# The end of a self-attention phase: exponentials, context work and the next LayerNorm in another order

## The chip, the cores and the metric

The kernel runs on one core of a Trainium2 chip. The metric is the device time of that core in microseconds, from runs that are not profiled; the median of three runs of the kernel before is 2554.23 us (2554.19 to 2556.33). One further execution was recorded by the profiler; all times inside the kernel come from that one.

## What is computed

Two transformer blocks follow each other on `x` of 8 x 512 x 512 in float32 (B = 8 sequences of N = 512 rows and H = 512 columns, 16 heads of 32), with a context of 8 x 77 x 512. Cut to what matters here (biases left out):

```python
# block 1 (phase "x"): cross attention of x to the context, adaptive LayerNorm
x = x + attention(ada_ln(x) @ Wq, ada_ln(ctx) @ Wkv) @ Wp
# block 2, phase "a": self-attention with modulation and a gate
q, k, v = split((ln(x) * (1 + scale_a) + shift_a) @ W_qkv)
x = x + gate_a * (softmax(q @ k.T * 32 ** -0.5) @ v @ W_proj)
# block 2, phase "c": cross attention to the context again
q_c = ln(x) @ W_qc
k_c, v_c = split(ln(ctx) @ W_kvc)
x = x + softmax(q_c @ k_c.T * 32 ** -0.5) @ v_c @ W_cproj
# block 2, phase "m": MLP 512 -> 2048 -> 512 with gelu, modulation and gate
```

The change lies where phase "a" ends and phase "c" begins.

## The kernel before

The four phases run one after the other. `x` lives in DRAM between them, one tensor per phase and sequence (`xa_b`, `xc_b`); in SBUF there are three slots of 128 x 4 x 512 (the pool `xres`), and `next_x` (L143 to L149) loads the next sequence in a fixed order into the next slot. Two of the three slots hold the running sums of exponentials (`sums`, `sum_a` in the profile) through the self-attention. The first load of phase "c", `x_c`, takes the slot of the first sum.

**Order of the work.** In phase "a" every engine's instructions keep the order in which the Python text makes them (`tc.manual_schedule(engines=None)`). Each engine takes its own in that order and waits by semaphores. The loads and stores that are issued from SyncE (SP) keep their order too, those of GpSimd (POOL) stand among POOL's additions, and two weight loads are issued from ScalarE (ACT). In phase "c" the compute engines keep the written order as well.

**Self-attention.** The work is cut into 32 groups: one sequence and four heads each (`Group`, L973). Per group the score tiles S^T are made (128 keys x 4 heads x 512 queries, four tiles k = 0 to 3, each in two halves of 128 x 1024), copied to SBUF as `e_a`, and the maxima go through DRAM (`spread`, L1027). Then:

- `shift(k)` (L1042): POOL issues for each half of tile k a DMA that adds the negated maxima, read from DRAM and broadcast, onto `e_a`. 512 KB are read and written for each half, eight halves for a group.
- `exp(k)` (L1052): ACT takes the exponential of both halves in place (L1054).
- `add_up(k)` (L1056): running sum of the tiles, on POOL for k = 1 and 2 and on VectorE (DVE) for k = 3 (L1061).
- `outputs(k)` (L1065): 4 products of `e_a` with the values into `o_ps_a` in PSUM (L1071).
- `total` and `finish` (L1078, L1087): sum over keys by a product with ones (L1082), reciprocal (L1089) and product (L1092), which gives `oT_a`.

`project(b, t)` (L952) makes row tile t of the output projection: 4 products (L302), a bias addition on DVE that frees the PSUM tile (L960), and through `flush` two operations on POOL (L963, L964) and a store from SP (L967).

**Context work beside it.** `ContextC` makes the keys and values of the context for phase "c": `values(t)`, five row tiles (L349), each copied from PSUM by ACT (L354) and stored to DRAM by SP (L355); after the fifth, one load from SP brings all values back as `cv_c` with 77 partitions (L467). `keys(j)` (L469) makes a block of the keys in two pieces (512 and 104 columns, L473) with an ACT evacuation each (L478). All these, the projection and `total` share two PSUM banks (tag `m`) in turn.

**The last group.** Groups overlap inside the main loop. The last one, of sequence 7, has nothing behind it, and its steps are written out by hand after the loop, beside values 2, 3 and 4 and keys 0 and 1 of the context. `g` is this group, `prev` the one before it, `past` the one before that. `next_x(nc.sync)` loads `x_c` of sequence 0. `ln_rows` (L252) is the LayerNorm of phase "c" for it, a generator with these pieces: statistics of row tiles 0 and 1 (L259, L260); of tiles 2 and 3; the first six small operations of the inverse root (L221 to L230); the rest of them with the offset (L243); then four ACT operations that normalise one row tile each (L248). `ln_T` of phase "c" then transposes the rows on TensorE (`lnT_ps_c`, L281), with a copy by ACT for each block (L283), and phase "c" goes on with keys 2 of the context and the first queries (`s_ps_qc`, L510).

The lines that put each wait into the code are few:

```python
# L469 keys(j): a yield after each product, the evacuation after the last
for at, n, cT in ((0, H, self.cT), (H, RL, self.last)):
    pk = ps_m.tile([P, H], F32, tag="m", ...)
    for k in range(KC):
        nc.tensor.matmul(pk[:, :n], lhsT=self.w_k[:, k, ts(j, P)], rhs=cT[:, k, :], ...)
        yield
    evac = nc.scalar.activation(self.kT[:, j, at : at + n], pk[:, :n], ...)
```

`values(t)` has one yield, between its products and its copy. `pump(gen, n)` takes n such steps, `run(gen)` takes the rest.

Of the kernel before, what the change touches and what calls it, by code (L numbers as in the profile page):

```python
# [29 lines left out]
def tile_pixart_block(ctx: ExitStack, tc: tile.TileContext, a: dict, out: bass.AP):  # L30
    nc = tc.nc
    x, ctx_in, cond = a["x"], a["ctx_1024"], a["cond_1024"]
    B, N, _ = x.shape
    S = ctx_in.shape[1]
    NT = N // P
# [13 lines left out]
    def load_w(name, u, rows=False, pool=wpool, queue=nc.sync):  # L49

        t = pool.tile([P, KC, H], F32, tag="w", name=f"w_{name}_{u}")
        w = a[name]
        src = w[ts(u, H), :] if rows else w[:, ts(u, H)]
        queue.dma_start(out=t, in_=src.rearrange("(k p) f -> p k f", p=P))
        return t
# [26 lines left out]
    gate_a = dram.tile([B, H], F32, name="gate_a")  # L82
# [6 lines left out]
    def run(gen):  # L89
        while True:  # L90
            try:
                next(gen)
            except StopIteration as stop:
                return stop.value
# [48 lines left out]
    def next_x(queue=nc.scalar):  # L143

        if len(x_sb) < len(x_order):
            ph, b = x_order[len(x_sb)]
            t = xpool.tile([P, NT, H], F32, tag="x", name=f"x_{ph}{b}")
            x_sb[ph, b] = t
            return queue.dma_start(out=t, in_=x_src[ph][b].rearrange("(t p) d -> p t d", p=P))  # L149
# [65 lines left out]
    def rsqrt_pieces(var, eps, nm, n):  # L215
        rows = var.shape[0]
        v = small.tile([P, CT], F32, tag="ln_v", name=f"lnv_{nm}")
        y = small.tile([P, CT], F32, tag="ln_y", name=f"lny_{nm}")
        t = small.tile([P, CT], F32, tag="ln_t", name=f"lnt_{nm}")
        v, y, t = v[:rows, :n], y[:rows, :n], t[:rows, :n]  # L220
        nc.vector.tensor_scalar(v, var, eps, None, ALU.add)  # L221

        nc.vector.tensor_scalar(
            y.bitcast(I32), v.bitcast(I32), -0.5, RSQRT_SEED, ALU.mult, ALU.add
        )
        nc.vector.tensor_scalar(v, v, -0.5, None, ALU.mult)
        for i in range(3):
            nc.vector.tensor_tensor(t, y, y, ALU.mult)
            nc.vector.tensor_tensor(t, t, v, ALU.mult)
            nc.vector.scalar_tensor_tensor(y, t, 1.5, y, ALU.add, ALU.mult)  # L230
            if i == 0:
                yield
        return y

    def normalise(dst, src, mv, y, i, rows):
        nc.vector.tensor_scalar(
            dst, src, mv[:rows, i, 0:1], y[:rows, i : i + 1], ALU.subtract, ALU.mult
        )

    def offsets(mv, y, n):  # L240

        off = small.tile([P, CT], F32, tag="off", bufs=2, name="off")[:, :n]
        nc.vector.scalar_tensor_tensor(off, mv[:, :n, 0], -1.0, y, ALU.mult, ALU.mult)  # L243
        return off

    def normalise_s(dst, src, off, y, i, rows):

        nc.scalar.activation(  # L248
            dst, src, AF.Identity, bias=off[:rows, i : i + 1], scale=y[:rows, i : i + 1]
        )  # L250

    def ln_rows(nm, b, eps, vector=False):  # L252


        xb = x_sb[nm, b]
        mv = small.tile([P, NT, 2], F32, tag="mv", name=f"mv_{nm}{b}")
        for t in range(NT):
            bn = small.tile([P, 6], F32, tag="st", name=f"st_{nm}{b}_{t}")
            nc.vector.bn_stats(bn, xb[:, t, :])  # L259
            nc.vector.bn_aggr(mv[:, t, :], bn)  # L260
            if t % 2:
                yield
        y = yield from rsqrt_pieces(mv[:, :, 1], eps, f"{nm}{b}", NT)
        off = offsets(mv, y, NT)
        yield
        for t in range(NT):
            if vector:
                normalise(xb[:, t, :], xb[:, t, :], mv, y, t, P)
            else:
                normalise_s(xb[:, t, :], xb[:, t, :], off, y, t, P)  # L270
            yield
# [27 lines left out]
    def mm_N(ps, w, xT, cols):  # L299

        for k in range(KC):
            nc.tensor.matmul(  # L302
                ps, lhsT=xT[k][:, cols], rhs=w[:, k, :], start=(k == 0), stop=(k == KC - 1)
            )
            yield

    def gate_rows(gate, b, pool, nm, bufs=2):
        g = pool.tile([P, H], F32, tag="gate", bufs=bufs, name=f"gate_{nm}{b}")
        nc.sync.dma_start(out=g, in_=gate[b].partition_broadcast(P))
        return g  # L310
# [28 lines left out]
    with tc.tile_pool(name="ps_s", bufs=2, space=PSUM, reuse_waits="tile") as ps_s:  # L339
# [539 lines left out]
        def self_phase(w, bo_row, work, work_2, ctx_c):  # L879
# [4 lines left out]
            st = [dict(xT=[], v={}, o=[], q={}, k={}, x={}) for _ in range(B)]  # L884
# [9 lines left out]
            def flush(part):  # L894

                while later[part]:
                    later[part].popleft()()
# [6 lines left out]
            def load_tile(b, t, queue=nc.scalar):  # L904
                xr = work.tile([P, H], F32, tag="xr", bufs=4, name=f"xr_a{b}_{t}")
                queue.dma_start(out=xr, in_=x_src["a"][b][ts(t, P), :])
                st[b]["x"][t] = xr
# [44 lines left out]
            def project(b, t):  # L952
                if t == 0 and b + 1 < B:
                    st[b]["g"] = gate_rows(gate_a, b, work, "a")
                pr = ps_m.tile([P, H], F32, tag="m", name=f"proj_ps_a{b}_{t}")
                for i, _ in enumerate(mm_N(pr, w_o, st[b]["o"], ts(t, P))):
                    if i == KC - 1:
                        xr = st[b]["x"].pop(t)
                        tmp = work.tile([P, H], F32, tag="res", bufs=3, name=f"res_a{b}_{t}")
                        nc.vector.tensor_tensor(tmp, pr, bo_row, ALU.add)  # L960

                        def add():
                            nc.gpsimd.tensor_tensor(tmp, tmp, st[b]["g"], ALU.mult)  # L963
                            nc.gpsimd.tensor_tensor(xr, xr, tmp, ALU.add)  # L964

                        def store():
                            nc.sync.dma_start(out=x_dst["a"][b][ts(t, P), :], in_=xr)  # L967

                        later[0].append(add)
                        later[1].append(store)  # L970
                    yield
# [136 lines left out]
            def pump(gen, n):  # L1108
                for _ in range(n):
                    next(gen, None)  # L1110
# [103 lines left out]
            g = groups[-1]  # L1214
# [16 lines left out]
            value = ctx_c.values(2)  # L1231
            next(value)
            prev.total()
            run(value)
            prev.finish()
            work_2.release()
            kv = tc.alloc_tile_pool(name="kv_c", bufs=1, side="right", reuse_waits="tile")
            ctx_c.room(kv)
            next_x(nc.sync)
            rows = ln_rows("c", 0, 1e-6)  # L1240
            fills = [ctx_c.values(3), ctx_c.values(4), ctx_c.keys(0)]
            for k in range(NT):
                g.exp(k)
                if k:
                    g.add_up(k)
                g.outputs(k)
                if k == 0:
                    st[g.b]["g"] = gate_rows(gate_a, g.b, work, "a")
                    for t in range(NT):
                        load_tile(B - 1, t, nc.sync)  # L1250
                if k < len(fills):
                    run(fills[k])
            w_c = [load_w("L1_xcond_W_qc", 0, queue=nc.scalar)]
            w_c.append(load_w("L1_xcond_W_cproj", 0, queue=nc.scalar))
            run(ctx_c.keys(1))
            g.total()
            g.finish()
            run(rows)
            for t in range(NT):
                run(project(B - 1, t))  # L1260
                flush(0)
                flush(1)
            return w_c, kv

        class Modulation:
# [66 lines left out]
        with tc.tile_pool(name="work_a", bufs=2, reuse_waits="tile") as work, tc.tile_pool(  # L1332
            name="ps_a", bufs=2, space=PSUM, reuse_waits="tile"
        ) as ps_m, tc.tile_pool(
            name="ps_o", bufs=2, space=PSUM, reuse_waits="tile"
        ) as ps_o, tc.manual_schedule(engines=None):
            w_l1 = [load_w("L1_xcond_W_qkv", u) for u in (2, 0, 1)] + [load_w("L1_xcond_W_proj", 0)]
            ctx_c = ContextC(load_w("L1_xcond_W_kvc", 1), work, c_mv)
            w_c, kv = self_phase(w_l1, load_row("L1_xcond_b_proj", 0, "bo"), work, work_2, ctx_c)
# [297 lines left out]
```

## Time and profile before

| what | value |
|---|---|
| median of three runs | 2554.23 us |
| the profiled execution's own time | 2556.85 us |
| its span, first to last instruction | 2555.1 us |
| granted TensorE clock, mean | 0.99 |
| phase "a", first to last product `o_ps_a` | 508.7 to 1344.2 us |
| exponentials of the last group begin | 1319.23 us |
| `oT_a` of the last group begins | 1353.73 us |
| projection tile 2 begins | 1360.72 us |
| first transposes of `x_c` (block 0) | 1367.26 us |
| first queries of phase "c" (`s_ps_qc`) | 1374.91 us |

The profile lists an instruction by line, engine, operation and tile (`out<-in`), with its start from the beginning of the span and its duration. PE is TensorE; PEld is its weight load, which can overlap; a float32 product shows as two records in this kernel, so four products of a projection tile are eight. A bracket `[1.68 <-DVE res_a L960]` says that the engine was idle for 1.68 us before the instruction, and what ended it. SPq, ACTq and POOL with DMA_DIRECT2D are issues of transfers, not the transfers.

### The profile page before, as it was taken

The page shows a single profiled execution, that of the slowest core. Times are in us where ns is not written, and L with a number is a line of the kernel's source. Part 1 is how long each engine was busy: PE and PEld are TensorE (multiplying, and loading weights), DVE is VectorE, ACT ScalarE, POOL GpSimd, SP SyncE. Part 2 cuts the span into 40 slices and gives each one's busy share as a digit, 9 for nine tenths or more (in the row PEclk, how much of TensorE's full clock was granted, in tenths as well). Part 3 has the DMA queues.
Part 4 walks back from the last instruction along what each step waited for, and adds up shares of the span by engine and source line. Part 5 has one row for each costly group of instructions (what it writes and reads, how often), then busy time and mean ns, then how long its engine had stood idle before and what let it go on. Part 6 is the DMA issues. An engine that isn't in the chain of part 4 may idle for free. (4 is left out here: it accounts for less than half of the span.)

```text
span 2555.1 us, 35387 instructions
## 1 busy us (share of the span) xinstructions
PE 2437.6 (95%) x13205; PEld 1562.6 (61%) x13205; DVE 1776.1 (70%) x3230; ACT 1224.9 (48%) x2083; POOL 1103.1 (43%) x982
## 2 busy tenths in 40 slices
PE   7999999989999999999988999998999999999998
PEld 3577776323333333333325777777888888888887
DVE  3588886478788888887756888887546545555553
ACT  1466665477676776767643666662121121121220
POOL 2245452277776877768663445445102102012011
PEclk9899999999999999999999999999999999999999
DMA  7323323499999899999995213133111011011010
GB/s 259 135 51 95 89 27 74 102 180 193 198 179 205 183 199 195 180 199 180 216 210 171 72 34 67 18 64 98 36 35 38 33 39 38 25 34 49 20 35 25
DMA packets 116676, 273.44 MB, mean 107 GB/s; under 512 B 12722, under 2 KB 29186, under 8 KB 116378
## 3 DMA queue, kind: packets, MB, share of 16 engines
q0 software_dynamic: 46368, 151.06, 33.0%
q1 hardware_dynamic: 64197, 108.37, 12.6%
q10 hardware_dynamic: 5941, 11.76, 1.3%
q8 instruction: 104, 1.70, 0.3%
q14 instruction: 66, 0.54, 0.1%
HBM read 234.78 MB, written 44.76 MB: 109 GB/s over the span
## 5 line engine op out<-in xcount | busy, mean ns | idle before, releaser
L1546 POOL TENSOR_TENSOR res_m<-res_m,gate_m 128x256 f32<-128x256 f32 x64 | 52.1, 814 | 665.1 <-DVE res_m L1544 665.1
L1045 POOL DMA_DIRECT2D e_a<-mxd_a x256 | 250.4, 2060 | 157.9 <-DMA mxd_a<-mxT_a 148.6
L1054 ACT ACTIVATE e_a<-e_a 128x1024 f32<-128x1024 f32 x256 | 265.1, 1058 | 98.4 <-DMA e_a<-mxd_a 98.0
L1009 ACT COPY e_a<-sT_a 128x1024 f32<-128x1024 f32 x256 | 254.2, 1010 | 91.0 <-DVE mx_a L1011 49.0
L1480 ACT ACTIVATE hT<-hT,bcol 128x512 f32<-128x512 f32 x128 | 91.9, 721 | 237.0 <-DVE hT L1455 228.9
L1061 POOL TENSOR_TENSOR sum_a<-e_a,e_a 128x1024 f32<-128x1024 f32 x64 | 150.2, 2363 | 105.8 <-ACT e_a L1054 105.4
L1011 DVE TENSOR_TENSOR mx_a<-sT_a,mx_a 128x1024 f32<-128x1024 f32 x128 | 150.9, 1216 | 33.6 <-PE sT_a L991 27.9
L1061 POOL TENSOR_TENSOR sum_a<-sum_a,e_a 128x1024 f32<-128x1024 f32 x64 | 171.2, 2686 | 5.3 <-ACT e_a L1054 5.3
L991 PE MATMUL sT_a<-qT_a,kT_a 32*128 32x512 f32 x1024 | 151.4, 640 | 17.7 <-ACT e_a L1009 16.1
L1071 PE MATMUL o_ps_a<-e_a,v 128*32 128x512 f32 x1024 | 152.9, 608 | 12.8 <-ACT e_a L1054 12.8
L1447 PE MATMUL q_ps_h<-x_m,w_L_xcond_W_mlp 128*128 128x256 f32 x512 | 132.3, 381 | 0.0
L1447 PE MATMUL q_ps_h<-xT_m,w_L_xcond_W_mlp 128*128 128x256 f32 x512 | 131.6, 380 | 0.0
L294 PE MATMUL q_ps_a<-xnT_a,w_L_xcond_W_qkv 128*128 128x512 f32 x256 | 124.1, 613 | 7.6 <-ACT xnT_a L914 7.6
L1089 DVE RECIPROCAL rz_a<-z_ps_a 128x512 f32<-128x512 f32 x32 | 107.4, 3357 | 31.9 <-PE z_ps_a L1082 31.9
L1447 PE MATMUL q_ps_h<-x_m,w_s 128*128 128x256 f32 x512 | 121.9, 381 | 5.3 <-DVE w_s L1401 4.6
L302 PE MATMUL proj_ps_a<-w_L_xcond_W_proj,oT_a 128*128 128x512 f32 x256 | 118.1, 605 | 3.1 <-DVE res_a L960 1.7
L294 PE MATMUL k_ps_a<-xnT_a,w_L_xcond_W_qkv 128*128 128x512 f32 x256 | 120.5, 608 | 0.0
L302 PE MATMUL v_ps<-w_L_xcond_W_qkv,xnT_a 128*128 128x512 f32 x256 | 119.7, 611 | 0.0
L991 PEld LDWEIGHTS sT_a<-qT_a,kT_a 32*128 32x128 f32 x1024 | 42.4, 183 | 117.7 <-ACT e_a L1009 51.9
L1447 PE MATMUL q_ps_y<-w_L_xcond_W_mlp,h_s 128*128 128x256 f32 x512 | 113.1, 379 | 0.0
L1447 PE MATMUL q_ps_y<-w_L_xcond_W_mlp,hT 128*128 128x256 f32 x512 | 113.1, 379 | 0.0
L1447 PE MATMUL q_ps_y<-w_t,h_s 128*128 128x256 f32 x512 | 111.8, 379 | 0.0
(368 smaller groups left out, 5531.1 us busy)
## 6 DMA issues: line engine op xcount, KB each, us to landing
e_a<-mxd_a POOLq DMA_DIRECT2D x256, 512.0 KB, 11.7
xa<-res_x POOLq DMA_DIRECT2D x32, 256.0 KB, 5.2
xr_a<-xa SPq DMA_DIRECT2D x32, 256.0 KB, 6.1
xc<-xr_a SPq DMA_DIRECT2D x32, 256.0 KB, 8.6
x_c<-xc SPq DMA_DIRECT2D x8, 1024.0 KB, 5.1
w_L_xcond_W_mlp<-in_L_xcond_W_mlp_dram SPq DMA_DIRECT2D x8, 1024.0 KB, 6.9
xc<-res_c POOLq DMA_DIRECT2D x32, 256.0 KB, 5.0
x_m<-xc SPq DMA_DIRECT2D x8, 1024.0 KB, 5.4
```

What stands on the lines that cost most here:

```text
L294: nc.tensor.matmul(ps, lhsT=w[:, k, ts(j, P)], rhs=xT[k], start=(k == 0), stop=(k == KC - 1))
L302: nc.tensor.matmul(ps, lhsT=xT[k][:, cols], rhs=w[:, k, :], start=(k == 0), stop=(k == KC - 1))
L991: nc.tensor.matmul(sc[h // 2][:, h % 2, :], lhsT=kT[ts(h, HD), ts(k, P)], rhs=qT[ts(h, HD), :], start=True, stop=True,)
L1009: nc.scalar.copy(self.e[k][i], sc[i])
L1011: nc.vector.tensor_tensor(self.mx[1 - i], sc[1 - i], self.e[0][1 - i] if k == 1 else self.mx[1 - i], ALU.max,)
L1045: nc.gpsimd.dma_start(out=self.e[k][i].rearrange("p h n -> p (h n)"), in_=self.mxd[2 * i : 2 * i + 2, :] .rearrange("h n -> (h n)").partit ...
L1054: nc.scalar.activation(self.e[k][i], self.e[k][i], AF.Exp)
L1061: engine.tensor_tensor(sum_i, self.e[0][i] if k == 1 else sum_i, self.e[k][i], ALU.add)
L1071: nc.tensor.matmul(self.po[ts(h, HD), :], lhsT=vt[:, self.fc * P + h * HD : self.fc * P + (h + 1) * HD], rhs=self.e[k][h // 2][:, h % 2, : ...
L1089: nc.vector.reciprocal(r, self.pz)
L1447: nc.tensor.matmul(self.banks[n][:, half], lhsT=lhsT, rhs=rhs, start=(k == 0), stop=(k == len(pairs) - 1),)
L1480: nc.scalar.activation(dst, src, AF.Gelu_apprx_tanh, bias=bias_cols("L1_xcond_b_mlp1", 1, j))
```

## The change

```diff
             value = ctx_c.values(2)
             next(value)
             prev.total()
+            g.exp(0)
             run(value)
             prev.finish()
             work_2.release()
             kv = tc.alloc_tile_pool(name="kv_c", bufs=1, side="right", reuse_waits="tile")
             ctx_c.room(kv)
+            g.outputs(0)
+            st[g.b]["g"] = gate_rows(gate_a, g.b, work, "a")
+            for t in range(NT):
+                load_tile(B - 1, t, nc.sync)
+            fills = [ctx_c.values(3), ctx_c.values(4), ctx_c.keys(0)]
+            for k, fill in enumerate(fills, 1):
+                pump(fill, 4 if k == 3 else 1)
+                g.exp(k)
+                g.add_up(k)
+                run(fill)
+                g.outputs(k)
             next_x(nc.sync)
-            rows = ln_rows("c", 0, 1e-6)
-            fills = [ctx_c.values(3), ctx_c.values(4), ctx_c.keys(0)]
-            for k in range(NT):
-                g.exp(k)
-                if k:
-                    g.add_up(k)
-                g.outputs(k)
-                if k == 0:
-                    st[g.b]["g"] = gate_rows(gate_a, g.b, work, "a")
-                    for t in range(NT):
-                        load_tile(B - 1, t, nc.sync)
-                if k < len(fills):
-                    run(fills[k])
             w_c = [load_w("L1_xcond_W_qc", 0, queue=nc.scalar)]
             w_c.append(load_w("L1_xcond_W_cproj", 0, queue=nc.scalar))
             run(ctx_c.keys(1))
             g.total()
             g.finish()
-            run(rows)
+            rows = ln_rows("c", 0, 1e-6)
             for t in range(NT):
+                next(rows)
                 run(project(B - 1, t))
                 flush(0)
                 flush(1)
+            run(rows)
             return w_c, kv
```

The change has three parts.

1. **Exponentials ahead of copies.** On ACT the four pairs of exponentials of the last group now stand one place earlier: exp(0) ahead of the copy of values 2, exp(1) ahead of that of values 3, exp(2) ahead of that of values 4, exp(3) ahead of both evacuations of keys 0. TensorE's order is as before.
2. **The load later.** `next_x`, the load of `x_c`, stands on SP's queue behind the load of the gate, the four loads of `xr_a`, the last two stores of context values and the load of `cv_c`, directly ahead of a weight load (`W_mod`). Before, it stood ahead of all of these.
3. **LayerNorm between the projection's tiles.** On DVE the statistics of rows 0 and 1, those of rows 2 and 3, the first half of the inverse root and its second half now stand ahead of the bias addition (L960) of projection tiles 0, 1, 2 and 3 respectively. Before, all four pieces stood ahead of the first. The normalisation on ACT stands behind the projection in both.

Nothing is added to or taken from what is computed.

## Prediction

> **What bounds the kernel now.** The page comes first. TensorE is busy nearly all the time, so a gain has to be idle time of TensorE that goes away. The windows view puts such time where phase "a" ends: in columns of PE, PEld, DVE, ACT and POOL busy time, PE has 12 us less work in the last stretch of 200 us than in the one before.
>
> ```profile
> PE 2437.6 (95%) x13205; PEld 1562.6 (61%) x13205; DVE 1776.1 (70%) x3230; ACT 1224.9 (48%) x2083; POOL 1103.1 (43%) x982
> ```
> ```profile
> 1000.00:1200.00 200.00, 190.59 (x817) 62.99 (x816) 164.84 (x188) 142.81 (x160) 150.11 (x106) 1.00 0.96 192
> 1200.00:1400.00 200.00, 178.55 (x769) 72.08 (x767) 130.22 (x165) 101.66 (x138) 121.17 (x91) 0.97 0.83 195
> ```
>
> The chain of waits, taken over this stretch, names the holes (start, duration, what):
>
> ```profile
> 1329.65 3.62 PE cv_ps_c L349 x8
> 1333.78 1.07 ACT e_a L1054
> 1334.89 2.00 PE o_ps_a L1071 x8
> 1336.89 4.52 PE ckT_ps_c L473 x16
> 1341.82 0.91 ACT e_a L1054
> 1342.78 2.00 PE o_ps_a L1071 x8
> 1344.78 4.50 PE ckT_ps_c L473 x16
> 1349.28 1.04 PE z_ps_a L1082 x8
> 1350.34 3.37 DVE rz_a L1089
> ...
> 1360.07 0.61 DVE res_a L960
> 1360.72 7.13 PE proj_ps_a L302 x16
> 1367.98 0.69 DVE res_a L960
> 1368.71 0.67 PE lnT_ps_c L281 x4
> ```
>
> Each block of context work is followed by an exponential that begins only after it, because ACT takes the copy of that block first. At 1360.72 the projection restarts after a bias addition that stood behind the LayerNorm on DVE.
>
> What the exponentials may wait for instead is the shift transfer. The tile view of `e_a` has eight, the last issued at 1317.7 and landing 21.2 us later, at 1338.9; the semaphore records give all eight: 1314.3, 1317.5, 1323.0, 1325.8, 1329.0, 1332.3, 1335.6, 1338.9.
>
> ```profile
> L1045 POOL DMA_DIRECT2D e_a<-mxd_a x8: 887/2032/3255, 1309.2 to 1317.7; - x8
> DMA to landing us min/median/max: 5.1/11.6/21.2
> ```
>
> The load that moves will stand behind `cv_c`, where `W_mod` stands now. The DMA view around these two issues gives that place 15.0 us:
>
> ```profile
> cv_c<-cvd_c SPq DMA_DIRECT2D x1, 1232.0 KB
> w_L_xcond_W_mod<-in_L_xcond_W_mod_dram SPq DMA_DIRECT2D x1, 1024.0 KB, 15.0
> ```
>
> **What the Trainium skill says.** "DMA: Bandwidth & Descriptors", section "Why a DMA increments its semaphore by 16 and not by 1": a transfer from SP uses the largest number of engines up to 16 that divides its slowest dimension; 77 rows give 11. The trace agrees: of `cv_c`'s increments, eleven come one by one between 1355.1 and 1356.9. So 11 engines carry 56 rows of 2 KB each, and a load behind it is done only when these are. Same page, "Issuing engines are not separate DMA queues": SP and ACT share the engines. It agrees: `cv_c`, issued at 1343.75, moves its first rows at 1347, when the first of ACT's two weight loads is nearly through. "TensorE: Matmul & The Clock Gate", section "What's actually happening": an idle window of about 3.4 us halves the clock. It agrees (windows view; PEclk is third from the end):
>
> ```profile
> 1293.20:1296.60 3.40, 0.86 (x4) 0.20 (x2) 3.30 (x5) 2.13 (x3) 3.24 (x4) 1.00 1.06 210
> 1296.60:1303.42 6.82, 4.74 (x22) 3.53 (x26) 3.21 (x5) 5.36 (x11) 6.74 (x5) 0.50 1.06 234
> 1358.03:1361.44 3.41, 1.73 (x5) 0.66 (x4) 2.89 (x14) 1.34 (x2) 0.69 (x1) 1.00 0.54 208
> ```
>
> A window with 0.86 us of work is followed by half clock for 6.8 us; one with 1.73 is not. The border is not sharp: one of 1.82 at 1399 is followed by 6.8 us of half clock too. Same page, "Architectural detail: the array is 16× 32×32, not 1× 128×128": DVE is a strict FIFO, which is what holds L960 at 1360 although its product was ready at 1355.
>
> **The change, part by part.**
>
> *Exponentials.* The order on PE stays: products of output k follow context block k. Output 0 starts when `z_ps_a` is through, 1319.7 (now 1320.35). Values 3 take 3.65 us, to 1325.3; the second half of exp(1) is bound by its landing, 1325.8 + 1.06 for one exponential = 1326.9, so output 1 ends at 1327.9 (one half is 0.95). Values 4: 1331.6; exp(2) 1332.3 + 1.06, with wake-up 1333.5; output 2 ends at 1334.5 (now 1336.8). Keys 0, 4.57: 1339.1; exp(3) 1338.9 + 1.06 = 1340.0; output 3 ends at 1341.0 (now 1344.7). Then keys 1 and z as now, 5.6, and reciprocal and product 4.1: `oT_a` is done at 1350.8 instead of 1354.4, **3.6 us earlier**. New waits on PE: values 3 for the copy of values 2 (done 1319.3, wanted 1321.6) and keys 0's second piece for that of values 4 (1334.0, wanted 1337.9) cost nothing; keys 1 waits for an evacuation behind exp(3) (1340.75, wanted 1341.0), covered by 0.3 us, and later it would delay `oT_a` one for one. The adds of POOL and DVE follow the exponentials; DVE's last ends at 1341.3 with z wanted at 1345.6.
>
> *LayerNorm.* With `x_c` present, four pieces between the tiles save the projection its stall: first addition 1.6 us after `oT_a` instead of 5.6. But normalisation then ends later, since its second half waits for tile 2. From the rows of now: two statistics 1.61; addition to PE 0.74; tile 2 to its addition 3.74; addition 0.60; six small operations 1.18; 0.20 to ACT; four normalisations 2.93: **11.0 us** from the first statistic to the last normalised row, whatever came before.
>
> *The load.* On SP it leaves 1 MB ahead of gate, `xr_a` and two stores, and is itself behind `cv_c`, which waits for the last store of values. That landed at 1343.6 and `cv_c` went at 1343.75. The four 256 KB transfers that now fill `x_c`'s place (gate and three `xr_a`) are through when `x_c` was, 1339.1; the fourth and the two stores take 0.65 each, as they do now: 1341.1. `cv_c` goes at 1341.2, 2.5 us earlier. ACT's two weight loads, 2 MB ahead of it, go when keys 0 are through: 1339.1 instead of 1341.44, 2.3 earlier. So the place behind `cv_c` lands 2.4 us earlier than `W_mod` did (1344.16 + 15.0 = 1359.2): **`x_c` lands at 1356.8**, 6 us after DVE is ready for it. No run shows this wait. Bounds: 4.4 MB (two weights, `cv_c`, `x_c`) from 1341.2 at 400 GB/s, the best rate of the trace (1339 to 1341), give 1352.2; no gain on `W_mod` gives 1359.2. I take 1356.8. Behind DVE's wait are all four L960; for them wait PE's tiles 2 and 3 and POOL's additions. `W_mod` behind it lands near 1359.6 and is read after 1405; `cv_c` near 1354.5, read at 1397; the next `x_c` near 1362, read at 1387.7; the gate and `xr_a`, now earlier, are first read with the addition of tile 0: all free. If one of these reads came before its landing, it would cost the difference, but the nearest has 25 us.
>
> *Sum.* 1356.8 + 11.0 = 1367.85; last transpose and copy of block 0 at 1368.25 (now 1368.33); block 1 need not wait for L960 of tile 3 (now to 1368.71), so block 3 is transposed at 1369.45 instead of 1370.04: **-0.6**. PE is busy from there on, so the rest shifts by this. *Clock.* PE has tiles 0 and 1 done at 1355.3 and tile 2 starts at 1359.2: 3.9 us idle, against 1.7 now. One or two windows with under 1.5 us of work follow from that for nearly any phase of the windows, then half clock for 3.4 to 6.8 us, partly in the idle time, with 7 us of products behind. Cost between 0 (no dip) and 3.4; I take **+1.4**. Total +0.8: profiled 2556.85 becomes 2557.65. The median is 2.6 below the profiled time; I move it alike: **2555.0**.
>
> **The rivals.** *Main case (0.5)*, the late load eats the gain: from -2.9 (landing at 1354.5, no dip) to +3.8 (one us late, 6.8 us at half clock), 2551.3 to 2558.0. *The load comes in time (0.2)*: five engines carry no `cv_c`, and the queue reached 400 GB/s. Landing at 1352.2, block 3 is transposed 12.65 later, 1364.85: -5.2, **2549.0**. Against it: about 285 GB/s from 1350 to 1360. *Slower (0.3)*: the wait of DVE costs more than the moved work gains. The clock record has one dip of 10.2 us, at 433; in PE-bound work that is 5.1. With a landing 1 us later: -0.6 + 1.0 + 5.1 = +5.5, **2559.7**. It decides from a second cold window after tile 2 on, or a landing after 1360. That the exponentials don't move is excluded for the order on ACT, but if other transfers hold the shifts, `oT_a` gains less; there are 6 us of slack to the load, so the time stays that of the main case.
>
> **How the numbers follow.** 0.2% is 5.1 us, about what a measurement of this kernel can tell from no change. Faster 0.2, within 0.5, slower 0.3, one case each. The range leaves out most of the fast case and the far end of the slow one: 2550.0 to 2560.5.
>
> **What would show it.** Right: `oT_a` near 1350, the first `st_c` near 1357 and waiting for the DMA of `x_c`, L960 of tile 0 after it, tile 2 at 1359, perhaps at half clock. Wrong: `st_c` straight behind `oT_a` (then faster), or tile 2 after 1363 (then slower).

## The result, and the profile after

The changed kernel takes 2561.14 us (median of 11 runs, 2558.09 to 2564.67) against 2554.19 us of the kernel before in the same series (11 runs, 2551.92 to 2559.63). The ratio is 1.0026, with a 95% interval of 1.0017 to 1.0035: slower by 7 us where the forecast was 2555.0, no change. The profiled execution took 2558.39 us, with a span of 2556.5.

Lines of after now sit one higher behind the change (`mod_ps` is L1287). Ahead of this stage TensorE runs for some 38 us at half clock in the profile before and for some 31 us in the profile after, and the end of the phase starts 3.0 us earlier after: the last transfer of maxima to DRAM (`mxd_a`, L1040) is issued at 1301.89 against 1304.89. All stages below are therefore counted from that issue. The **stretch** is the time from it to the first query of phase "c" (`s_ps_qc`), where TensorE is busy again for long: 70.0 us before, 74.6 after. Behind it both profiles need the same, 1180.2 and 1180.1 us.

The busy line of the page after, and the windows view (duration, then PE, PEld, DVE, ACT, POOL, granted clock third from the end):

```profile
PE 2433.2 (95%) x13205; PEld 1560.1 (61%) x13205; DVE 1782.5 (70%) x3230; ACT 1228.3 (48%) x2083; POOL 1102.8 (43%) x982
```
```profile
1200.00:1400.00 200.00, 175.60 (x744) 71.93 (x743) 128.30 (x157) 97.89 (x131) 117.45 (x88) 0.96 0.82 190
1355.77:1359.19 3.42, 3.17 (x4) 1.51 (x5) 3.32 (x8) 0.00 (x0) 3.07 (x3) 0.50 0.46 176
1369.43:1372.84 3.41, 3.28 (x10) 2.44 (x11) 1.34 (x2) 1.74 (x4) 3.33 (x3) 0.50 0.62 212
```

In the 200 us around the change PE is busy for 3.0 us less than before, and it has two windows at half clock that the profile before does not have there. Ahead of the first of them TensorE stands idle for 4.75 us, where it was 1.68 before (timeline of PE after):

```profile
1356.02 8.69 PE L302 MATMUL proj_ps_a<-w_L_xcond_W_proj,oT_a 128*128 128x512 f32 x16 [4.75 <-DVE res_a L960]
```

The tile view of `e_a` and the DMA view of this stage:

```profile
L1045 POOL DMA_DIRECT2D e_a<-mxd_a x8: 887/2035/3256, 1305.3 to 1313.9; - x8
DMA to landing us min/median/max: 4.9/11.7/21.0
```
```profile
x_c<-xc SPq DMA_DIRECT2D x2, 1024.0 KB, 16.2
```

Counted from the issue of the maxima, the shifts land 0.7 to 1.1 us earlier than before, and from the second half tile on each exponential now begins within 0.1 us of its landing: the last at 1334.84, 33.0 after the issue, against 37.7 (1342.62) for the same one before. `oT_a` is done 44.8 after the issue; before it was 49.5. So this part gained 4.8 us. Then the chain of waits of after:

```profile
1337.43 16.23 DMA x_c<-xc
1353.68 0.70 DVE st_c L259
...
1358.71 1.20 DVE lny_c L223
...
1360.11 1.15 DVE lnt_c L228
...
1361.64 0.60 DVE res_a L960
...
1362.35 1.27 DVE lnt_c L229
...
1363.84 1.13 DVE lnt_c L228
...
1365.58 2.94 ACT x_c L248 x4
...
1369.56 1.97 PE lnT_ps_c L281 x8
1371.53 5.02 PE ckT_ps_c L473 x16
```

DVE waits 7.0 us for `x_c`, where 6 were foreseen. What was not foreseen are operations on 128x4 elements that take over 1 us each. The timeline of DVE and of POOL at that place, in the profile after:

```profile
1358.71 1.19 DVE L223 TENSOR_SCALAR lny_c<-lnv_c 128x4 int32<-128x4 int32 x1
1360.02 1.23 DVE L228 TENSOR_TENSOR lnt_c<-lny_c 128x4 f32<-128x4 f32 x1
1362.35 1.26 DVE L229 TENSOR_TENSOR lnt_c<-lnt_c,lnv_c 128x4 f32<-128x4 f32 x1
```
```profile
1358.61 1.27 POOL L963 TENSOR_TENSOR res_a<-res_a,gate_a 128x512 f32<-128x512 f32 x1
1359.95 1.27 POOL L964 TENSOR_TENSOR xr_a<-xr_a,res_a 128x512 f32<-128x512 f32 x1
1362.32 1.26 POOL L963 TENSOR_TENSOR res_a<-res_a,gate_a 128x512 f32<-128x512 f32 x1 [1.09 <-DVE lnt_c L228]
```

Add start and duration: L223 ends at 1359.90, L963 at 1359.88; L228 at 1361.25, L964 at 1361.22; L229 at 1363.61, L963 at 1363.58. Each of these small operations ends 0.02 to 0.03 us after the POOL operation that was running when it started. Before, none of these additions was running yet, and the same operations took 0.15 to 0.17 (timelines of DVE and POOL before):

```profile
1357.86 0.17 DVE L223 TENSOR_SCALAR lny_c<-lnv_c 128x4 int32<-128x4 int32 x1
1358.14 0.15 DVE L228 TENSOR_TENSOR lnt_c<-lny_c 128x4 f32<-128x4 f32 x1
1358.33 0.16 DVE L229 TENSOR_TENSOR lnt_c<-lnt_c,lnv_c 128x4 f32<-128x4 f32 x1
```
```profile
1360.74 1.27 POOL L963 TENSOR_TENSOR res_a<-res_a,gate_a 128x512 f32<-128x512 f32 x1 [21.11 <-DVE res_a L960]
```

Below, the **hold** is this: an operation of DVE that ends only when POOL's does.

The Trainium skill has this: "SBUF — State Buffer", section "Terms", says that DVE and GpSimd share one pair of SBUF ports, locked for a whole instruction while the other engine blocks; section "Who interferes with whom" says that a DVE operation with two SBUF inputs contends with a GpSimd operation that reads SBUF, one with a single SBUF input outside a two-port mode does not, and that `tensor_scalar` can enter such a mode under conditions. The trace agrees as far as it goes: L228 and L229 (two inputs in SBUF) are held, and so is L223 (`tensor_scalar`), though a trace does not name the mode; the statistics L259 and the bias addition L960 (its other input is in PSUM) keep their 0.66 us beside L963 and L964. The profile of the kernel before shows it too, early in phase "x", in its timelines of DVE and POOL:

```profile
41.02 1.19 DVE L226 TENSOR_SCALAR lnv_x<-lnv_x 128x4 f32<-128x4 f32 x1
```
```profile
40.93 1.26 POOL L560 TENSOR_TENSOR sq_x<-w_L_xcond_Wq,sq_x 128x512 f32<-128x512 f32 x1
```

### The profile page after: what moved, and what is told of

It is laid out like the page before. It is cut to its first block, busy times and chain, and to the rows that moved or that the text cites. A ratio compares the mean times of both kernels' runs of the same rounds, so it can differ in the third digit from the quotient of the medians.

```text
span 2556.5 us, 35388 instructions
## 1 busy us (share of the span) xinstructions
PE 2433.2 (95%) x13205; PEld 1560.1 (61%) x13205; DVE 1782.5 (70%) x3230; ACT 1228.3 (48%) x2083; POOL 1102.8 (43%) x982
## 4 chain that ended last, share of the span: by engine, by line
PE 36%; issue 28%; DVE 14%; DMA 11%; POOL 6%; ACT 4%; POOLq 0%; SPq 0%; ACTq 0%; DVEq 0%
DMA e_a<-mxd_a 6%; PE s_ps_qx L510 4%; PE s_ps_qc L510 4%; PE proj_ps_a L302 3%; DVE mx_a L1011 3%; PE sT_a L991 2%; PE q_ps_a L294 2%; PE s_ps_oc L510 2%; PE s_ps_ox L510 2%; POOL res_m L1547 2%; DMA mxd_a<-mxT_a 2%; POOL xr L1548 2%; PE pT_ps_c L742 2%; PE pT_ps_x L742 2%; DVE tu_a L1022 2%
## 5 line engine op out<-in xcount | busy, mean ns | idle before, releaser
L991 PE MATMUL sT_a<-qT_a,kT_a 32*128 32x512 f32 x1024 | 149.6, 643 | 14.5 <-ACT e_a L1009 12.9
L1463 ACT COPY p_h<-q_ps_h 128x256 f32<-128x256 f32 x64 | 23.7, 370 | 183.4 <-PE q_ps_h L1448 183.4
```

What stands on the lines that cost most here:

```text
L991: nc.tensor.matmul(sc[h // 2][:, h % 2, :], lhsT=kT[ts(h, HD), ts(k, P)], rhs=qT[ts(h, HD), :], start=True, stop=True,)
```

## The experiments

The theory after the result: the late load takes back what the exponentials gained, and the pieces between the tiles do not make up for it, because POOL's additions now run beside them and hold DVE; half clock follows where TensorE stands idle. The rivals: half clock alone; the load alone; the exponentials cost something. Each time is given as a ratio to runs of the kernel before beside it, with its 95% interval; 0.1% is 2.6 us. A stretch is one profiled execution.

| run | ratio to the kernel before | stretch, us |
|---|---|---|
| changed kernel | 1.0026 (1.0017 to 1.0035) | 74.6 |
| e1 exponentials | 0.9983 (0.9977 to 0.9990) | 65.4 |
| e2 late load | 1.0020 (1.0012 to 1.0029) | 74.6 |
| e3 pieces between tiles | 1.0023 (1.0014 to 1.0033) | 73.1 |
| e4 a new version | 0.9977 (0.9970 to 0.9983) | 63.8 |
| e5 changed, no POOL additions | 1.0006 (0.9998 to 1.0014) | 70.7 |
| e6 changed, PE kept busy | 1.0019 (1.0012 to 1.0025) | 73.4 |
| e7 both of these | 1.0009 (1.0000 to 1.0018) | 70.9 |
| e8 exponentials, late load | 1.0022 (1.0013 to 1.0031) | 75.8 |
| e9 exponentials, pieces | 0.9996 (0.9988 to 1.0004) | 70.0 |
| e10 pieces, no POOL additions | 0.9994 (0.9986 to 1.0002) | 69.0 |
| e11 late load, three products | 1.0028 (1.0019 to 1.0037) | 72.3 |
| e12 a delay in place of the load | 1.0019 (1.0011 to 1.0026) | 75.3 |
| e13 the delay, three products | 1.0010 (1.0002 to 1.0019) | 74.8 |
| e14 late load, five products | 1.0013 (1.0006 to 1.0020) | 72.5 |

**e1, the exponentials alone** (against the changed kernel):

```diff
             ctx_c.room(kv)
+            next_x(nc.sync)
             g.outputs(0)
...
-            next_x(nc.sync)
...
             rows = ln_rows("c", 0, 1e-6)
+            run(rows)
             for t in range(NT):
-                next(rows)
                 run(project(B - 1, t))
...
-            run(rows)
```

> The exponentials ahead of the copies alone; x_c is loaded early and its LayerNorm stands ahead of the projection, as in the kernel before. If the step of the prediction on the exponentials holds (oT_a 3.6 us earlier and everything behind it moved alike), the time is 3 to 4 us below the kernel before, about 2550.6. If the exponentials themselves cost something (other waits on PE, transfers in each other's way), it is at or above 2554.

Measured 2549.21 against 2554.08, with the stretch 4.6 us shorter. The exponentials gain somewhat more than the 3.6 us that they were meant to, and no cost of theirs shows.

**e2, the late load alone** (against the kernel before):

```diff
             ctx_c.room(kv)
-            next_x(nc.sync)
-            rows = ln_rows("c", 0, 1e-6)
...
+            next_x(nc.sync)
             w_c = [load_w("L1_xcond_W_qc", 0, queue=nc.scalar)]
...
+            rows = ln_rows("c", 0, 1e-6)
             run(rows)
```

> The late load alone: x_c is issued behind cv_c, exponentials as before, the whole LayerNorm ahead of the projection as before. DVE then waits for x_c instead of starting 0.1 us behind oT_a (1354.4). If the late load is the main loss: +3 to +5 us against the kernel before, 2557 to 2559, with a wait of 2 to 4 us of DVE for the DMA of x_c. If the load is harmless (a landing by 1355): 2554 to 2555.

Measured 2559.93. DVE waits only 1.6 us for `x_c`, but tiles 2 and 3 then run at half clock, 10.08 us in place of 7.13 (timeline of DVE and chain of waits of e2):

```profile
1350.59 0.69 DVE L259 BATCH_NORM_STATS2 st_c<-x_c 128x6 f32<-128x512 f32 x1 [1.64 <-DMA x_c<-xc]
```
```profile
1356.98 10.08 PE proj_ps_a L302 x16
```

1.6 and 2.95 make the 4.6 us of the stretch.

**e3, the pieces between the tiles alone** (against the kernel before):

```diff
-            run(rows)
             for t in range(NT):
+                next(rows)
                 run(project(B - 1, t))
                 flush(0)
                 flush(1)
+            run(rows)
```

> The LayerNorm's pieces between the tiles of the projection alone; x_c early, exponentials as before. If the small operations of the inverse root are held up by POOL's additions (about 1.2 us each in place of 0.16), the pieces cost more than the stall they save: +0.5 to +2.5 us, 2555 to 2556.5, and L221, L223, L228, L229 show means near 1 us. If the small operations stay short: the normalised rows come 11 us after the first statistic in place of about 9 and the stall of tile 2 goes: -1.2 us or so, 2553.

Measured 2559.84, more than expected, and without any late load. L223 takes 1.26 us, and of L228 and L229 three take 1.12 to 1.26. This part alone costs as much as the late load does.

**e4, a version built on the theory** (against the changed kernel; the load early as in e1):

```diff
             run(ctx_c.keys(1))
+            rows = ln_rows("c", 0, 1e-6)
+            for _ in range(NT):
+                next(rows)
             g.total()
             g.finish()
-            rows = ln_rows("c", 0, 1e-6)
+            run(rows)
             for t in range(NT):
-                next(rows)
                 run(project(B - 1, t))
...
-            run(rows)
```

> A version meant to beat both: exponentials ahead, x_c loaded early, and the four DVE pieces of its LayerNorm placed behind keys 1 and ahead of total and finish, where DVE is idle and POOL has no additions; the four normalisations on ACT stand ahead of the projection. If the theory (late load and POOL's hold on DVE are the losses) is right: small operations at 0.15 to 0.2 us, no stall ahead of tile 2, 4.5 to 6 us below the kernel before, about 2549. If the loss lies in the exponentials or in clock dips alone: 2553 or more.

Measured 2547.8 against 2554.08, 6 us below the kernel before, and by the two ratios 12 below the changed one. The LayerNorm's DVE work is done ahead of `rz_a`, where POOL has nothing to do: every small operation takes 0.16 to 0.17. Most of the gain is that of e1: from e1 to e4 it is 1.4 us, with intervals that overlap, so what the new place of the LayerNorm is worth beside e1 is not shown by the times (the stretch is 1.6 us shorter). The chain of waits has the projection in one piece:

```profile
1348.94 0.70 DVE oT_a L1092
1349.69 11.43 PE proj_ps_a L302 x26
1361.24 0.69 DVE res_a L960
```

**e5 to e7, the two suspects taken away from the changed kernel**, one by one and together:

```diff
 # e5 and e7, in project(b, t)
-                        later[0].append(add)
+                        if b == B - 1:
+                            xr = tmp
+                        else:
+                            later[0].append(add)
 # e6 and e7, where phase "a" ends
                 run(project(B - 1, t))
+                if t in (1, 3):
+                    keep_busy(4 if t == 1 else 3)
```

e5 and e7 leave out the gate and the residual of sequence 7, POOL's L963 and L964 of the four tiles. `keep_busy(n)` makes n products of `ident` with `oT_a` into a PSUM tile of its own.

> The changed kernel with the gate and the residual of sequence 7 left out (L963 and L964 for its four tiles; the product with its bias is stored as it is), so that POOL has nothing to do beside the LayerNorm's small operations. If POOL's additions hold DVE: all small operations at 0.15 to 0.2 us, the second half of the inverse root takes 1.2 us instead of 3.2, the second clock dip becomes unlikely; tile 2 still runs at half clock. 2 to 3.5 us below the changed kernel (2561.1), about 2558.5. If the long small operations have another cause: they stay near 1.2 us and the time at 2561.

> The changed kernel with seven products added that nobody reads: four of 128x512 behind projection tile 1 and three behind tile 3, in TensorE's two idle stretches. If clock dips are the whole loss: no half clock between 1340 and 1400, tile 2 in 3.7 us instead of 5.5, and 3 us or more off the changed kernel, 2558 or less. If POOL's hold on DVE is as large: tile 2's product is ready earlier, but its addition L960 still waits for DVE until the first half of the inverse root is through, so only the second dip's 1.2 us goes: about 2560.

> Both at once: the changed kernel without the gate and residual of sequence 7 and with the seven products added. If the two causes are as large as the trace says and each hides part of the other (tile 2 waits for whichever is later), more goes than by either alone: 1.8 us of tile 2, 2.0 of the second half, 1.2 of the second dip, 5 in all, 2556, near the kernel before plus 2. If one of them is the only cause, this run is no better than the better one alone.

Their traces separate the causes, counted in each from its own first statistic:

| | start of L960 of tile 2 | last row normalised | from there to the first query |
|---|---|---|---|
| prediction | 6.1 | 11.0 | 6.5 |
| changed kernel: hold and half clock | 7.88 | 14.82 | 7.95 |
| e6: hold alone | 7.88 | 14.82 | 6.42 |
| e5: half clock alone | 7.72 | 12.63 | 6.42 |
| e7: neither | 6.07 | 10.98 | 7.5 |

The first line is worked out from the prediction: 1.61 + 0.74 + 3.74; its sum; and block 3 at 1369.45 with 4.87 us from there to the first query, as in the profile before, less 1367.85.

In timelines of DVE: e6, where tile 2 is made at full clock and the addition has to wait nonetheless, for the held operations ahead of it, and e7:

```profile
1361.89 0.68 DVE L960 TENSOR_TENSOR res_a<-proj_ps_a,row_L_xcond_b_proj 128x512 f32<-128x512 f32 x1
```
```profile
1365.93 0.69 DVE L960 TENSOR_TENSOR res_a<-proj_ps_a,row_L_xcond_b_proj 128x512 f32<-128x512 f32 x1 [0.67 <-PE proj_ps_a L302]
```

The bracket says it: in e7 DVE waited for tile 2, in e6 (no bracket) tile 2 waited for DVE. The hold makes 3.8 us by itself, the half clock of tile 2 1.65, and both together no more than the hold, since they lie side by side. In times: 5 us go with the additions (1.0026 to 1.0006, intervals apart), more than the 2 to 3.5 expected; 2 go with half clock (1.0019, an interval that overlaps); and e7, which was to be better than e5, is not. Its last column says why in part: the three products behind tile 3 end at 1371.7 and hold the transposes up, for which the first row is ready in time, so that 1.1 us are lost again; and `x_c` landed 0.7 us later in its profile than in e5's.

The edit of e5 does a second thing. With the additions gone POOL makes its products for phase "c" (L557 to L560) at 1345.8 to 1350.9, and no longer beside the first DVE work of that phase. Behind the first query e5 needs 1179.2 us, the changed kernel 1180.0, so up to 0.8 of the 5 us may come from there; the kernel before was not run without its additions. The 3.9 us by which the stretch is shorter lie ahead of that: 2.2 in the LayerNorm, 1.5 in the half clock behind it, and 0.1 in the landing of `x_c`.

**e8 and e9, pairs.** e8 is the changed kernel with `run(rows)` ahead of the projection, e9 the changed kernel with the load early as in e1.

> Exponentials ahead and the late load, with the LayerNorm in one piece ahead of the projection. If the landing of x_c sets the end whatever came before, the 4.9 us that the exponentials gained alone are gone here: first statistic 51.8 us after the last store of the maxima as in the changed kernel, TensorE idle for some 8 us ahead of tile 2 and at half clock behind it, 2559.5 to 2562, no better than the late load alone (2559.9). If the parts add up: 2554.1 - 4.9 + 5.8 = 2555.

> The changed kernel with the load early, as in the kernel before; exponentials ahead and the pieces between the tiles stay. If the parts add up: -4.9 + 5.8 = +0.9 against the kernel before, with L223, L228 and L229 near 1.2 us and the stretch from the last store of the maxima to the first query of phase c at 70 - 4.6 + 3.0 = 68.4. If the load alone is the loss in the changed kernel: 4 us or more below the kernel before.

e8 measured 2559.15 against 2552.90: no better than the late load without the exponentials (1.0022 and 1.0020). So the landing takes the gain whole: DVE waits 7.3 us in e8 and 1.6 in e2 (timeline of DVE of e8):

```profile
1354.33 0.69 DVE L259 BATCH_NORM_STATS2 st_c<-x_c 128x6 f32<-128x512 f32 x1 [7.25 <-DMA x_c<-xc]
```

e9 measured 2552.03 against 2552.58, near the sum of its parts, -4.9 + 5.8. Its profiled execution was the longest of its 13 (2557.31) and has two half-clock stretches in the 70.0 us, the first of them ahead of `oT_a`, so that figure is high. From e9 to the changed kernel only the load moves, and 0.3% are lost with it; from e8 to the changed kernel only the pieces move, and no difference shows.

**e10, e3 without the additions** (edit of e5 on e3):

> The pieces between the tiles alone (load early, exponentials as before), with the gate and the residual of sequence 7 left out. If POOL's hold is what makes the pieces dear: small operations at 0.16, the last row normalised 2 us or more earlier than with the additions, stretch to the first query at or below that of the kernel before (70.0), time 0 to 1.5 us below it. If the order itself costs (normalisation can't end before tile 2 is added): stretch near 71 to 72 and 1 to 2 us above the kernel before even without POOL.

Measured 2551.6 against 2552.58; last row normalised 13.07 us after the first statistic, 15.40 in e3. Without the hold the pieces between the tiles do no harm; a clear gain they are not either, with 1.0 in the interval.

**e11 to e14, what the late load costs by.** e11 and e14 are e2 with three or five unread products behind projection tile 1. e12 is the kernel before with a delay of DVE and no transfer moved, e13 the same with three products:

```diff
             g.finish()
+            idle = work.tile([P, N], F32, tag="rz", bufs=1, name="idle")
+            for _ in range(4):
+                nc.vector.tensor_tensor(idle, st[B - 1]["o"][0], st[B - 1]["o"][0], ALU.mult)
             run(rows)
```

> The late load alone, with three products of 128x512 added behind projection tile 1 that nobody reads, so that TensorE does not stand idle there. If the half clock behind the idle time is the larger part of what the late load costs (10.1 us for tiles 2 and 3 in place of 7.1): these take 7.1 again, the stretch to the first query falls from 74.6 to 71.7, and the time is 1.5 to 2.5 us above the kernel before in place of 5.8. If the wait for x_c is the larger part: 4 us or more above it.

> The kernel before with four products of 128x512 on VectorE, read by nobody, between oT_a and the LayerNorm: 2.6 us later for every step behind, with no transfer moved. If the late load costs by its wait and the idle TensorE: the same half clock behind the longer idle time and 4 to 6 us above the kernel before. If it costs by the transfer's place: no more than 2.6 us.

> The same delay with three unread products of 128x512 on TensorE behind projection tile 1. If half clock is part of the cost of the delay: 2.6 us above the kernel before and 1.5 to 3 us below the delay alone. If keeping TensorE busy changes nothing: the same time as the delay alone.

> The late load alone with five unread products in place of three, so that TensorE has work until VectorE frees the tile. If half clock counts: 2 to 3 us above the kernel before (wait of x_c alone). If it doesn't: 5 to 6 us above it, as the late load alone (+5.8) and with three products (+6.4).

The delay of 2.8 us costs 0.19%, what the late load costs (0.20%), and in its chain tiles 2 and 3 take 10 us again; in e14, with work for TensorE all the while, they take 7 (the chain counts 6.87 of it):

```profile
1362.68 10.04 PE proj_ps_a L302 x16
```
```profile
1359.76 6.87 PE proj_ps_a L302 x16
```

So a wait of DVE of this size is enough for the loss, and the transfer's place among the others is not needed for it. In the traces more than half of it is half clock: 2.9 of 5.3 us in e12, 2.95 of 4.6 in e2. The times say so less clearly: e13 (where one window of half clock is left and the tiles take 8.83 us) and e14 lie below e12 and e2, with intervals that overlap, and e11 does not lie below at all, though its profile shows tiles 2 and 3 in 7.13 us. How large the share of half clock is in the timed runs stays open.

## Why the prediction was wrong, step by step

- **Exponentials, 3.6 us earlier: right in kind, somewhat small.** 4.8 after, 4.6 in e1. The last shift landed 32.9 us after the maxima's issue in place of 34.0. POOL had issued it 12.0 us after that issue in place of 12.9, which makes 0.9 of the 1.1 us; why POOL was earlier is not shown.
- **The load: right, with luck in the number.** `x_c` was to land 51.9 us after that issue (1356.8 - 1304.9) and landed 51.8 after it. Two misses cancel in this: it was issued 35.5 us after the maxima, where the prediction's sum has 36.9 (1344.16 - 2.4), and took 16.2 us to land, where it has 15.0. That it then eats the whole gain of the exponentials is what e8 shows.
- **LayerNorm, the step that failed: "six small operations 1.18" in the sum of 11.0 us.** Their duration was read where POOL stood idle and carried to a place where POOL runs L963 and L964 of the tiles just added, which the change itself had put beside them. The prediction names POOL's additions only as work that waits for L960, and puts what they do to DVE at nothing. The first six small operations stand in no sum: unheld they fit in beside tile 2 (e7). Measured: 3.5 us for the first six (1358.06 to 1361.56), 3.2 for the six that the sum has (1362.16 to 1365.38), and 14.8 us in all. With the additions left out and PE kept busy the chain takes 10.98 us (e7): every other term of the sum was right.
- **Clock, +1.4: half right.** The first dip came as foreseen (the products of tile 2 took 5.25 us, 1356.02 to 1361.27, where e6 needs 3.70) but cost nothing of its own, because DVE was held until 1361.56 anyway. The hold brought another: PE idles while the normalisation is late, and the transposes and keys behind run at half clock, 7.95 us to the first query instead of 6.5.
- **The sum.** Predicted stretch without clock 70.0 - 0.6 = 69.4 (1356.8 + 11.0 is 1367.8, not 1367.85, which changes nothing). Landing -0.1, L960 of tile 2 +1.8, second half +2.0, the second dip +1.5: 74.6, as measured. For the 1.8 the half clock of tile 2 is nearly enough alone (1.65 in e5), and the hold alone is enough (e6). With its clock term the prediction has 70.8, so 3.8 us were missing, 3.5 of them in the second half and the second dip. The timed medians lie 7 us apart; to which step the other 2.4 us belong the runs don't tell, since each profile is one execution with half-clock stretches of its own.
- **The rivals.** "Slower" had the right sign and nearly the right size (2559.7), and of its two conditions one came true: a second cold window after tile 2. But that window followed from the hold, and the late landing it named did not occur, so its size was luck.
- **The signs.** All that was named as a sign of being right came true: counted on the clock of the profile before, `oT_a` was done at 1349.7, the first `st_c` came at 1356.7 behind the DMA of `x_c`, and tile 2 began at 1359.0, at half clock. The sign of a slower kernel, tile 2 after 1363, stayed away. The step that failed lies behind all of these, so none could show it.

With the one term put right by taking its cause away (e5), the stretch is 70.7 us, where the prediction with its clock term has 69.4 + 1.4 = 70.8, and the ratio is 1.0006, some 1.5 us above the kernel before: within a microsecond of the forecast of 2555.0, though the interval goes from 0.5 us below the kernel before to 3.6 above it.

## What to carry to other kernels

A duration is only worth something together with what the other engine of the pair does at that time: before moving small VectorE operations, look at what POOL runs at the new place, and search the trace for the longest instance of the same line, not its median: for L223 in phase "x" of the profile before these are 1.19 and 0.17 us. A chain of dependent operations of 0.16 us each is a bad thing to put there, since after each gap the next POOL operation catches it again, four times for over 1 us in the changed kernel; ahead of the additions (e4) none was held. And a load moved behind others can set the start of all work behind it: here the gain ahead of it (e1) was worth nothing (e8), because the load did not come earlier too.

## What the runs showed of the hardware that was not expected

A 128x4 operation on VectorE (`tensor_tensor` or `tensor_scalar`) took as long as the rest of the 1.27 us POOL operation that it met, up to 1.26 us against 0.16; thirteen of them, with L960 in between, took 7.5 us in the changed kernel (1358.06 to 1365.54; L960 is 0.6 of it), and 2.4 in e4. Nor are only small operations longer beside POOL: L566, of 128x512, takes 1.75 us in the profile before, where POOL makes its products for phase "c" beside it, and 0.68 in e10, where POOL has made them earlier. In e2 a wait of 1.6 us was followed by 6.8 us of half clock: TensorE stood idle for 3.4 us there in place of 1.7, and the loss, 4.6 us, was nearly three times the wait.
